# Attention and depthwise convolution on one core: the fourth pair's q and k copied through GpSimd's queue, two conv tiles added by accumulating transfers, one tap fewer before the last reciprocals

## The chip, the cores and the metric

The kernel runs on one core of a Trainium2 chip. The metric is the device time of one execution in microseconds. Before the change it is 2937.13 us, the median of three runs (2937.04 to 2937.74); the profiled execution took 2939.7 us, with a span of 2937.6 us in the trace. All times below that say where something stands are microseconds from the start of that span.

## The reference

The input x has 16 images of 384 channels and 32 x 32 pixels in float32. Two residual layers follow one another.

```python
# layer 0: attention with 8 heads of 48 channels over 1024 pixels
x = x + attention(group_norm(x, 32 groups), w_qkv, w_proj, b_proj)
# layer 1: one 7x7 filter per channel, padding 3, stride 1
x = x + depthwise_conv(group_norm(x, 32 groups), symmetrised(w_conv))
```

`group_norm` takes mean and variance over 12 channels and all pixels. `attention` is softmax(q k^T / sqrt(48)) v for each head, then a 384 x 384 projection with a bias. `symmetrised` is the mean of the filter and its three rotations by 90 degrees.

## The kernel before

An image is three tiles of 128 channels x 1024 pixels. The eight heads are worked as four **pairs**; a pair's two heads lie on rows 0 to 47 and 64 to 111 of a tile. A unit u is one pair of one image (u = 4 b + pair, 64 in all) and has 16 steps.

**TensorE, step by step.** A step makes scores (L463), ScalarE takes their exponential (L471), and TensorE multiplies by v (L479). Steps go in batches of eight: eight score steps, a slot for other work, eight steps with v, another slot. In the slots lie the q and k of the next pairs (L412, copied out of PSUM by ScalarE at L419), v (L438), the projection of the image before (L532, which reads o), and ScalarE's normalisations (L334). The matmuls of an image follow one another almost without a gap.

**The fourth pair's q and k.** Each of the three tiles that `qk_step` makes holds 48 rows for each of two heads and, in the rows left over (48 to 63 and 112 to 127), a third of the two heads of the fourth pair. `qk_rest` (L425 to L431) gathers these 6 x 16 rows into a tile of their own by six transfers of 128 KB from SBUF to SBUF. They are issued on SyncE's queue when the third q and k of an image have been emitted. Right after them the next image's x is loaded into the same buffer by three transfers (L155), on GpSimd's queue from image 2 on. The unit that reads the gathered rows begins 32 steps later.

**Softmax sums.** v carries a column of ones, so that one row of the product is the softmax sum. `sums_out` sends it through HBM into a compact tile (L497, L498, SyncE). VectorE takes the reciprocals (L504, `rec`), SyncE writes them to HBM (L506, inv<-rec) and, when that has landed, reads them back spread over 64 rows each (L509, inv<-inv). VectorE then multiplies o by inv (L515); after the fourth pair SyncE moves o's rows back to the packed order (L520), and the projection can read them. [...]

**VectorE.** Nearly all its work is the convolution: 49 instructions ("taps", L597) per tile, each a multiply-add of a shifted tile into x1. An order written by a small planner decides where everything else stands between the taps: `after(wait, cost, f)` puts f into the order when VectorE's planned clock gets there, and `catch_up` fills the time between with taps. The planner's clocks are fixed estimates.

**The end.** Four tiles of the last two images, `PE_TILES` = (14,2), (14,1), (15,2), (15,1), are convolved on TensorE (L705), of (14,1), called `SHARED`, only the last four pixel rows. `conv_on_pe_end` (L717 to L721) adds the PSUM result to x1 on VectorE (L720), and `conv_end` (L610) sends x1 to the output on GpSimd's queue. The tile (15,0) is convolved on VectorE into two accumulators that are added last (L860). In `fast_finish` the last pair is divided without going through HBM: two matmuls (L558) spread the sums, VectorE takes a 128 x 512 reciprocal (L560) and multiplies (L561), TensorE finishes the projection (L569), VectorE adds the residual (L578) and takes statistics (L234), TensorE averages these over groups (L302), and then the last image's tiles are normalised, stored and read back shifted (L674, L681) for TensorE. Two taps stand before the second L560 (L1140).

The pools that matter: `tpool` has 2 buffers of 128 x 1024 (squares and inv), `ps_s` 3 PSUM tiles of 128 x 1024, `xpool` 1 buffer for x.

Of the kernel before, what the change touches and what calls it, by code (L numbers as in the profile page):

```python
# [10 lines left out]
F32 = mybir.dt.float32  # L11
I32 = mybir.dt.int32
AF = mybir.ActivationFunctionType
ALU = mybir.AluOpType
AX = mybir.AxisListType

P = 128
# [27 lines left out]
def kernel(  # L45
# [25 lines left out]
    nc = tc.nc  # L71

    B, C, H, W = x.shape
    N = H * W
# [35 lines left out]
    def run(general):  # L110
        tag = "g" if general else "f"
        with ExitStack() as stack:
# [3 lines left out]
            def pool(name, bufs, **kw):  # L116
                return stack.enter_context(tc.tile_pool(name=f"{name}_{tag}", bufs=bufs, **kw))
# [8 lines left out]
            tpool = pool("tpool", 2)  # L126
# [10 lines left out]
            xds, shs, pss, mats, psums = {}, {}, {}, {}, {}  # L137
            PE_K = [NK - 1, NK - 2]

            PE_TILES = [(b, k) for b in (B - 2, B - 1) for k in PE_K]  # L140
            SHARED = None if general else (B - 2, PE_K[1])
# [3 lines left out]
            def flat(t):  # L145
                return t.rearrange("p h n -> p (h n)")
# [274 lines left out]
            def qk_rest(b):  # L421

                u = NP * b + NK
                qks[u] = qkpool.tile([P, 2, N], F32, tag="qk", name=f"qk_{u}")
                for t in range(NK):  # L425
                    for j in range(2):
                        r = 64 * j
                        nc.sync.dma_start(
                            qks[u][r + 16 * t : r + 16 * t + 16],
                            qks[NP * b + t][r + D : r + 64],  # L430
                        )  # L431
# [123 lines left out]
            def divide_at_once(u, h):  # L555
                half = os_[u][:, h * HALF : (h + 1) * HALF]
                ps = ps_o.tile([P, HALF], F32, tag="acc", name=f"ps_sum_{u}_{h}")
                nc.tensor.matmul(ps, lhsT=late["masks"][:, 7, :], rhs=half, start=True, stop=True)  # L558
                inv = tpool.tile([P, N], F32, tag="t", name=f"inv_{u}_{h}")[:, 0:HALF]
                nc.vector.reciprocal(inv, ps)  # L560
                nc.vector.tensor_tensor(half, half, inv, ALU.mult)  # L561

            def proj_part(b, o, ts):
                if o not in pps:
                    pps[o] = psum(f"ps_proj_{b}_{o}")
                for t in ts:
                    lhsT = wp[:, t, o * P : (o + 1) * P] if t < NK else late["w3"][:, o * P : (o + 1) * P]
                    for h in range(2):
                        nc.tensor.matmul(  # L569
                            pps[o][:, h, :],  # L570
                            lhsT=lhsT,
                            rhs=os_[NP * b + t][:, h * HALF : (h + 1) * HALF],
                            start=(t == 0),
                            stop=(t == NP - 1),
                        )

            def residual(b, o):
                nc.vector.scalar_tensor_tensor(  # L578
                    halves(x1s[b, o]), pps.pop(o), bp[:, o : o + 1], halves(x1s[b, o]), ALU.add, ALU.add
                )  # L580
# [9 lines left out]
            def conv_tap(b, k, dy, dx, dst=None):  # L590
                (oy, iy), (ox, ix) = region(dy, dx)
                if (b, k) == SHARED:
                    oy = slice(oy.start, min(oy.stop, SPLIT))
                    iy = slice(iy.start, oy.stop - oy.start + iy.start)
                dst = x1s[b, k] if dst is None else dst
                acc = dst.rearrange("p (h w) -> p h w", w=W)[:, oy, ox]
                nc.vector.scalar_tensor_tensor(  # L597
                    acc,
                    xn1s[b, k].rearrange("p (h w) -> p h w", w=W)[:, iy, ix],
                    wsym[:, k, dy + PAD, dx + PAD : dx + PAD + 1],  # L600
                    acc,
                    ALU.mult,
                    ALU.add,
                )

            def conv_end(b, k):
                if (b, k) == SHARED and not late.get("shared"):
                    late["shared"] = True
                    return
                nc.gpsimd.dma_start(  # L610
                    out[b, k * P : (k + 1) * P].rearrange("p h w -> p (h w)"), x1s.pop((b, k))
                )
# [104 lines left out]
            def conv_on_pe_end(b, k):  # L717
                c = slice(SPLIT * W if (b, k) == SHARED else 0, N)
                dst = x1s[b, k][:, c]
                nc.vector.tensor_tensor(dst, flat(pss.pop((b, k)))[:, c], dst, ALU.add)  # L720
                conv_end(b, k)  # L721

            def exact_step(u, i):
# [95 lines left out]
            def us_tap(dy, dx):  # L819
                late_us = 0.02 if clock > last_image else 0.0  # L820
                rows = H - abs(dy)
                if tuple(active[0][0:2]) == SHARED:
                    rows = min(H - max(0, dy), SPLIT) - max(0, -dy)
                return (rows * (W - abs(dx)) + (128 if len(active) > 1 else 268)) / 955 + late_us

            def tap():

                while len(active) < NK and chains:
                    active.append([*chains.popleft(), 0])
                if not active:  # L830
                    return 0.0
                b, k, n = active[0]
                if (b, k) == LONE:
                    active.append(active.pop(0))
                    return tap_of_two(b, k, active[-1])
                took = us_tap(*TAPS[n])
                conv_tap(b, k, *TAPS[n])
                c = active.pop(0)
                c[2] += 1
                if c[2] < len(TAPS):  # L840
                    active.append(c)
                else:
                    conv_end(b, k)
                return took

            def tap_of_two(b, k, c):

                n = c[2]
                c[2] += 1
                if n == 1:  # L850
                    late["sum2"] = opool.tile([P, N], F32, tag="o", name=f"sum2_{b}_{k}")
                    nc.vector.tensor_scalar(
                        late["sum2"], xn1s[b, k], wsym[:, k, PAD, PAD : PAD + 1], None, ALU.mult
                    )
                elif n < len(TAPS):

                    tn = n if n > 1 else 1
                    conv_tap(b, k, *TAPS[tn], late["sum2"] if n % 2 else None)
                else:
                    nc.vector.tensor_tensor(x1s[b, k], x1s[b, k], late["sum2"], ALU.add)  # L860
                    active.remove(c)
                    conv_end(b, k)
                return (950 + 128) / 955
# [246 lines left out]
            def conv_piece(n=0):  # L1110
                nonlocal clock
                b, k, h, part = pe_conv[n]
                del pe_conv[n]
                while (b, k, h, 1) not in shs and pe_loads:
                    loads(1)
                conv_on_pe(b, k, h, part)
                clock += 2.0 if (b, k) == SHARED else 6.2
                if part == 1:
                    loads(2)
                if (h, part) == (1, 1):  # L1120
                    after(6.0, 1.2, lambda: conv_on_pe_end(b, k))
# [13 lines left out]
            def fast_finish(b):  # L1135
                nonlocal clock, vclock
                late["tail"] = b == B - 1

                proj_part(b, 0, (NP - 2,))
                tap(), tap()  # L1140
                divide_at_once(NP * b + NP - 1, 1)
                for o in range(1, NK):
                    proj_part(b, o, (NP - 2,))
                x1_stats[b] = Stats(f"x1_{b}")
                tap(), tap()
                for o in range(NK):
                    proj_part(b, o, (NP - 1,))
                    residual(b, o)
                    x1_stats[b].channels(x1s[b, o], o)
                clock += 2 * US_PROJ + 1.0  # L1150
                vclock = clock + 4.0
# [14 lines left out]
            for b, n0, size in [  # L1166
# [35 lines left out]
                if ending:  # L1202
                    catch_up(clock)
                    assert not invs and not waiting
                    fast_finish(b)
                else:
                    other(n0 + size, True)
# [4 lines left out]
                if b == B - 1:  # L1212
# [10 lines left out]
                    if once("ones", r >= 32):  # L1223
                        t = opool.tile([P, N], F32, tag="o", name="masks_1")
# [74 lines left out]
```

## Time and profile before

| what | value | where |
|---|---|---|
| time | 2937.13 us | median of 3 runs |
| TensorE busy with matmuls | 2900.6 us, 99% | busy times |
| VectorE busy | 2575.7 us, 88% | busy times |
| ScalarE busy | 1442.0 us, 49% | busy times |
| GpSimd busy | 204.4 us, 7% | busy times |
| DMA engines, mean | 58 GB/s | the line of DMA shares |
| software queue (GpSimd's), hardware queue q1 (SyncE's) | 12.9% and 10.0% of the engines' span | DMA queues |
| qk copies, per image | 6 of 128 KB, issue median 587 ns, longest 3310 ns | line L428 |
| accumulating loads from GpSimd (L547) | issue 873 ns, landing 5.5 us | line L547 |

In the timeline an engine's name with a q (SPq, ACTq) is its queue issuing transfers; a number in square brackets is how long the engine stood idle before an instruction, with what ended the wait. In the chain of work each piece is what the next one waited for. Busy shares are means over stages with different limits, so the stages have to be looked at one by one.

### The profile page before, as it was taken

What the parts mean: (1) busy time and instruction counts of PE and PEld (TensorE: products, weight loads), DVE (VectorE), ACT (ScalarE), POOL (GpSimd) and SP (SyncE); (2) the same over time, 40 slices, a digit from 0 to 9 for tenths busy, and PEclk for the clock granted to TensorE, in tenths of its full rate; (3) what the DMA queues carried; (4) which work ended last, traced back from release to release, by engine and by line L of the source; (5) the groups of instructions that cost most, each with busy time, mean ns of one, the idle gap of its engine ahead of it and who ended that gap; (6) DMA issues with size and microseconds to landing.
All of it is one profiled execution on the core that took longest, in us unless ns stands there. A gap on an engine that the chain in (4) does not pass through costs nothing. (4 is left out here: it accounts for less than half of the span.)

```text
span 2937.6 us, 30293 instructions
## 1 busy us (share of the span) xinstructions
PE 2900.6 (99%) x11554; PEld 1171.1 (40%) x11554; DVE 2575.7 (88%) x2558; ACT 1442.0 (49%) x1724; POOL 204.4 (7%) x304
## 2 busy tenths in 40 slices
PE   8999999999999999999999999999999999999997
PEld 4343343434434343343434434343343434334332
DVE  5312998989999898999989999898999989899898
ACT  2545445464454545545464554546546365554510
POOL 3110004000100001000000100000010000100000
PEclk9999999999999999999999999999999999999998
DMA  7422022220302213022220301213031221301423
GB/s 298 116 26 62 16 35 77 41 63 21 82 16 42 69 23 82 16 43 62 42 62 24 83 21 35 69 29 75 16 64 41 42 63 28 83 16 35 119 65 110
DMA packets 72540, 169.84 MB, mean 58 GB/s; under 512 B 30416, under 2 KB 32352, under 8 KB 70848
## 3 DMA queue, kind: packets, MB, share of 16 engines
q0 software_dynamic: 29456, 96.08, 12.9%
q1 hardware_dynamic: 41328, 68.44, 10.0%
q10 hardware_dynamic: 1600, 3.28, 0.5%
q8 instruction: 93, 1.52, 0.2%
q14 instruction: 63, 0.52, 0.1%
HBM read 119.92 MB, written 29.36 MB: 51 GB/s over the span
## 5 line engine op out<-in xcount | busy, mean ns | idle before, releaser
L597 DVE SCALAR_TENSOR_TENSOR x<-xn,wsym,x 128x899 f32<-128x899 f32 (+11 forms) x2181 | 2371.7, 1165 | 105.4 <-ACT xn L334 105.4
L471 ACT ACTIVATE e<-ps_s 128x1024 f32<-128x1024 f32 x1024 | 952.3, 1054 | 54.8 <-PE ps_s L463 51.8
L463 PE MATMUL ps_s<-qk 48*128 48x512 f32 x4096 | 915.0, 596 | 2.2 <-ACT qk L419 2.2
L479 PE MATMUL acc<-e,v 128*64 128x512 f32 x4096 | 907.2, 595 | 0.0
L463 PEld LDWEIGHTS ps_s<-qk 48*128 48x128 f32 x4096 | 375.5, 185 | 537.9 <-ACT e L471 259.8
L479 PEld LDWEIGHTS acc<-e,v 128*64 128x64 f32 x4096 | 283.0, 137 | 608.2 <-issue 598.8
L412 PE MATMUL ps_qk<-x,wqk 128*128 128x512 f32 x1152 | 507.9, 597 | 2.4 <-DVE x L330 2.4
L490 ACT COPY o<-acc 128x512 f32<-128x512 f32 x128 | 75.2, 587 | 602.6 <-PE acc L479 602.6
L412 PEld LDWEIGHTS ps_qk<-x,wqk 128*128 128x128 f32 x1152 | 217.0, 191 | 289.6 <-issue 287.1
L438 PE MATMUL ps_v<-wv,x 128*128 128x384 f32 x768 | 252.0, 488 | 0.0
L532 PE MATMUL ps_proj<-o,wp 128*128 128x512 f32 x540 | 234.3, 592 | 1.5 <-DMA o<-o 1.5
L419 ACT COPY qk<-ps_qk 128x1024 f32<-128x1024 f32 x96 | 96.4, 1006 | 240.5 <-PE ps_qk L412 240.5
L438 PEld LDWEIGHTS ps_v<-wv,x 128*128 128x128 f32 x768 | 144.6, 190 | 109.6 <-ACT e L471 12.1
L515 DVE TENSOR_TENSOR o<-o,inv 128x1024 f32<-128x1024 f32 x63 | 77.1, 1224 | 115.1 <-DMA inv<-inv 79.3
L547 POOL DMA_DIRECT2D x<-in_x x45 | 39.2, 871 | 1831.4 <-ACT x L540 1698.8
L532 PEld LDWEIGHTS ps_proj<-o,wp 128*128 128x128 f32 x540 | 102.4, 190 | 128.1 <-issue 123.5
L447 ACT COPY v<-ps_v 128x384 f32<-128x384 f32 x128 | 55.1, 483 | 185.6 <-PE ps_v L438 185.6
L540 ACT ACTIVATE x<-ps_proj,bp 128x1024 f32<-128x1024 f32 x45 | 50.1, 1113 | 184.7 <-PE ps_proj L532 184.7
L334 ACT ACTIVATE xn<-x,sc_x 128x1024 f32<-128x1024 f32 x46 | 53.8, 1231 | 98.3 <-DMA sc_x<-gr_x 67.6
L705 PE MATMUL ps_conv<-sh,mat 128*32 128x480 f32 (+7 forms) x784 | 73.0, 527 | 1.5 <-DMA sh<-xd 1.5
L504 DVE RECIPROCAL rec<-sums 128x16 f32<-128x16 f32 x63 | 15.6, 248 | 54.3 <-DMA sums<-sum 54.3
L265 ACT ACTIVATE sq_x<-x,x_bs 128x1024 f32<-128x1024 f32 x45 | 51.2, 1139 | 21.0 <-DVE x_bs L947 21.0
(118 smaller groups left out, 517.6 us busy)
## 6 DMA issues: line engine op xcount, KB each, us to landing
x<-in_x POOLq DMA_DIRECT2D x90, 512.0 KB, 5.7
inv<-inv SPq DMA_DIRECT2D x126, 256.0 KB
out<-x POOLq DMA_DIRECT2D x48, 512.0 KB, 7.3
xs<-in_x POOLq DMA_DIRECT2D x42, 512.0 KB, 5.9
qk<-qk SPq DMA_DIRECT2D x96, 128.0 KB
o<-o SPq DMA_DIRECT2D x90, 64.0 KB
sh<-xd SPq DMA_DIRECT2D x36, 160.0 KB
sh<-xd ACTq DMA_DIRECT2D x20, 160.0 KB
```

The lines of the kernel that those rows point to most:

```text
L412: nc.tensor.matmul(ps[:, h, :], lhsT=wqk[:, k, s, t, :], rhs=xns[b][:, k, h * HALF : (h + 1) * HALF], start=(k == 0), stop=(k == NK - 1),)
L419: nc.scalar.copy(halves(qks[u][:, s, :]), ps)
L438: nc.tensor.matmul(ps[:, j, 0:C], lhsT=xns[b][:, k, t * P : (t + 1) * P], rhs=wv[:, k, :], start=(k == 0), stop=(k == NK - 1),)
L447: nc.scalar.copy(dst.rearrange("p (h d) -> p h d", d=D + 1)[:, :, 0:D], ps[:, j, 0:C].rearrange("p (h d) -> p h d", d=D),)
L463: nc.tensor.matmul(ps[:, j, :], lhsT=qks[u][r, 1, i * P : (i + 1) * P], rhs=qks[u][r, 0, h * HALF : (h + 1) * HALF], start=True, stop=True,)
L471: nc.scalar.activation(es[n], ps, AF.Exp, scale=SCALE)
L479: nc.tensor.matmul(accs[u, h][64 * j : 64 * j + 64, :], lhsT=v_of(u, i, j), rhs=e[:, j, :], start=(i == 0), stop=(i == NT - 1),)
L490: nc.scalar.copy(os_[u][:, h * HALF : (h + 1) * HALF], accs.pop((u, h)))
L515: nc.vector.tensor_tensor(os_[u], os_[u], invs.pop(u), ALU.mult)
L532: nc.tensor.matmul(ps[:, h, :], lhsT=wp[:, t, o * P : (o + 1) * P], rhs=os_[NP * b + t][:, h * HALF : (h + 1) * HALF], start=(t == 0), sto ...
L597: nc.vector.scalar_tensor_tensor(acc, xn1s[b, k].rearrange("p (h w) -> p h w", w=W)[:, iy, ix], wsym[:, k, dy + PAD, dx + PAD : dx + PAD + 1],
L705: nc.tensor.matmul(pss[b, k][CH * i : CH * (i + 1), h, :].rearrange("p (y x) -> p y x", x=W)[:, y0:, ox], lhsT=mats[k][:, i, d0 * KS + dx ...
```

## The change

Three edits. First, `qk_rest` issues its six copies on GpSimd's queue in place of SyncE's, so that SyncE's queue isn't held up by them. Second, for the tiles (14,2) and (15,2) ScalarE copies the PSUM result into a tile of `tpool`, and a transfer that accumulates, issued by GpSimd, adds it to x1 in place of VectorE; the output transfer then waits for that transfer. (14,1) and (15,1) stay with VectorE. Third, one tap instead of two stands in front of the second reciprocal of `fast_finish`; the tap isn't dropped, the planner puts it in later.

```diff
                     for j in range(2):
                         r = 64 * j
-                        nc.sync.dma_start(
+                        nc.gpsimd.dma_start(
                             qks[u][r + 16 * t : r + 16 * t + 16],
                             qks[NP * b + t][r + D : r + 64],
                         )
...
                 dst = x1s[b, k][:, c]
-                nc.vector.tensor_tensor(dst, flat(pss.pop((b, k)))[:, c], dst, ALU.add)
+                src = flat(pss.pop((b, k)))[:, c]
+                if (b, k) in (SHARED, PE_TILES[-1]):
+                    nc.vector.tensor_tensor(dst, src, dst, ALU.add)
+                else:
+
+                    t = tpool.tile([P, N], F32, tag="t", name=f"conv_{b}_{k}")
+                    nc.scalar.copy(t, src)
+                    nc.gpsimd.dma_start(dst, t, accum_op=ALU.add)
                 conv_end(b, k)
...
                 proj_part(b, 0, (NP - 2,))
-                tap(), tap()
+                tap()
                 divide_at_once(NP * b + NP - 1, 1)
```

## The prediction

> **What bounds the kernel now.** I read the busy times first, then the chain that ended last, then the timeline of the stages that the three edits touch. TensorE is busy 99% of the span, and from one load of x to the next (L155) most images take 175.10 us whatever else happens, so until the last image TensorE sets the pace and only its stalls can be won or lost. The end is different. The chain of work from 2829.55 on runs like this:
>
> ```profile
> 2829.55 3.27 DVE inv L560
> ...
> 2833.66 6.25 PE ps_proj L569 x10
> ...
> 2853.73 6.26 DMA sh<-xd
> 2860.00 0.24 issue
> 2860.24 10.74 PE ps_conv L705 x93
> ...
> 2878.42 1.14 DVE x L720
> ...
> 2902.80 1.13 DVE x L720
> ...
> 2923.27 1.24 DVE x L860
> ```
>
> It starts with the second reciprocal of the last pair on VectorE, goes over to TensorE and the shifted loads, and from 2872 to the last output is VectorE alone, tap after tap. Two of its links are the additions L720 that the change takes away. TensorE ends its last convolution at 2917.45 and VectorE its last instruction at 2925.63, so VectorE is the one to relieve. Why is the reciprocal so late?
>
> ```profile
> 2819.91 9.64 DVE L597 SCALAR_TENSOR_TENSOR x<-xn,wsym,x 128x930 f32<-128x930 f32 x9
> 2829.47 3.35 DVE L560 RECIPROCAL inv<-ps_sum 128x512 f32<-128x512 f32 x1
> 2824.67 1.02 PE L558 MATMUL ps_sum<-o,masks 128*128 128x512 f32 x2
> 2828.96 1.02 PE L569 MATMUL ps_proj<-o,mat 128*128 128x512 f32 x2
> 2833.66 0.70 PE L569 MATMUL ps_proj<-o,mat 128*128 128x512 f32 x1 [3.68 <-DVE o L561]
> ```
>
> Its input is ready at 2824.67 + 1.02 = 2825.69, but taps are in front of it until 2829.47: VectorE is 3.78 us behind, and TensorE stands for 3.68 us. VectorE's last stall before that is at the first inv of the last image, and from there to the reciprocal it is never idle, so the whole of that lag comes from here:
>
> ```profile
> 2724.33 7.67 SPq L428 DMA_DIRECT2D qk<-qk  x6
> 2732.10 0.53 SPq L506 DMA_DIRECT2D inv<-rec  x1
> 2740.03 1.12 SPq L509 DMA_DIRECT2D inv<-inv  x2
> 2728.13 0.24 DVE L504 RECIPROCAL rec<-sums 128x16 f32<-128x16 f32 x1
> 2744.67 1.23 DVE L515 TENSOR_TENSOR o<-o,inv 128x1024 f32<-128x1024 f32 x1 [6.45 <-DMA inv<-inv]
> ```
>
> rec is done at 2728.37, but SyncE is inside the six copies until 2732.0, and the 8 KB of inv<-rec then need 7.9 us behind them. Without copies on the way the same path is short: at 2658.33 the issue of inv<-rec is followed by inv<-inv after 1.43 us, and rec to L515 takes 2664.27 - 2658.05 = 6.2 us.
>
> [...] from 2721 to 2725 the outputs of GpSimd's queue alone move 406 GB/s, from 1330 to 1335, when x's load shares the engines with two qk copies, the table of stretches shows 180 GB/s at a DMA share of 0.98. [...] the trace has accumulating loads at L547, 5.5 us to land, but none from SBUF.
>
> **The copies.** From SyncE six issues per image go away (median 587 ns each, 3.5 us; with the wait for the third copy of ScalarE they span 10 us). inv<-rec in the last image can be issued at 2728.4 instead of 2732.1[...]. inv must land by 2738.2 (= 2744.67 - 6.45) for the full gain: 9.8 us after rec, against 6.2 us on a free path and with some 2 MB of other transfers under way. I take 6.45 with a lower bound of 3. A first reciprocal, at 2810.78, has its input at 2804.47 + 1.12 = 2805.6 and so passes on at most 5.2 us; that still suffices, as the second needs 3.74 - 1.03 = 2.7.
>
> In images 1 to 14 VectorE waits 3 to 6 us at the same place, and then about 5 us for ScalarE's xn at the next image, where a gain is lost again. Only two stalls of TensorE hang on it: 0.69 and 0.77 us at 1092 and 1443, where the projection waits for o. There rec stands behind taps, 8 us and more after its sums were sent for, so a VectorE that is 4 us ahead removes both: -1.5 us. A third stall, 1.05 us at 273.55, comes from ScalarE waiting 7.52 us for a scale whose small transfer runs beside the first qk copies; on GpSimd's queue they come after it. I count half: -0.5 us.
>
> What it adds is on GpSimd: six issues, at the 530 ns of an x load 3.2 us per image, on an engine busy 7%. Four of them go out while it waits idle (5.98 us before L155 at 1325.07). The last two wait for ScalarE's copy L419, which ends 0.75 us after the load could start, and take 1.06 us, so behind them **x is issued 1.9 us later**. ScalarE normalises x at L334 after eight exponentials, and here is the slack:
>
> ```profile
> 1325.88 7.44 ACT L471 ACTIVATE e<-ps_s 128x1024 f32<-128x1024 f32 x8
> 1334.85 1.24 ACT L334 ACTIVATE x<-x,x_sc 128x1024 f32<-128x1024 f32 x1 [1.53 <-DMA x<-in_x]
> 1336.38 2.53 ACT L334 ACTIVATE x<-x,x_sc 128x1024 f32<-128x1024 f32 x2 [0.30 <-DMA x<-in_x]
> 1338.91 0.59 ACT L490 COPY o<-acc 128x512 f32<-128x512 f32 x1
> ```
>
> Its waits for x in the 14 images are 1.28, 0.38, 1.41, 1.88, 1.73, 1.52, 0.63, 0.47, 0.38 and five near zero. The image with 1.73 takes 175.10 us all the same, so about 1.7 us are free. Is x later by the 1.9 us? Now it is issued first, runs at about 340 GB/s, and then collides with the two copies and falls to 180. [...] I take no loss, with bounds from 0 to 2 us of delay.
>
> **The additions.** Two L720 leave VectorE's chain: 1.14 + 1.13 = 2.27 us. ScalarE gets two copies of 128 x 1024 out of PSUM, about 1.0 us each as at L419, at a time when it does nothing but issue loads. GpSimd gets two accumulating issues of about 0.9 us and stands until each has landed, 5 to 8 us, before it can issue that tile's output. Behind it in its queue is only the next output: for (15,2) the addition stands at 2902.73, so its output can go at about 2912, and the next outputs come after 2920. PSUM is freed about as before. I put all this at nothing.
>
> **The tap.** The reciprocal moves up by one tap, 1.03 us, but the tap comes back at the end. With VectorE late, the chain moves by -1.03 and the end by +1.03; with VectorE early it costs 1.03, since the reciprocal then waits for TensorE anyway.
>
> **The sum at the end.** With inv early the reciprocal starts at about 2825.73, TensorE's projection at 2830.0 (its own earlier matmuls end at 2829.98), 3.66 us sooner. Everything down to 2872 follows TensorE and moves with it, VectorE's stalls of 2.75, 1.67, 1.01 and 1.78 us included. VectorE ends at 2925.63 - 3.66 + 1.03 - 2.27 = 2920.73, so -4.9 us. With -1.5 and -0.5 this makes -6.9 us: 2937.1 - 6.9 = 2930.2.
>
> **The rivals.** (1) *inv's wait stays*: other transfers hold it as long. For it: in the last image 1 MB of stores lies in SyncE's ring and the residual's loads move into the same time. Against it: 3.7 us of the delay are plain issue order. Then the tap nets to nothing, and 2937.1 - 2.3 = 2934.8 is left. A mixture, with x late by 1 us, lies in the same place: the five waits above 1.2 would exceed 1.7 by 4.3 us together, 2934.5. (2) *GpSimd's queue makes x late*. For it: [...] SyncE's copies took up to 3.3 us each to issue[...]. With 2 us of delay the nine waits exceed 1.7 by 12.4 us and the five others by 0.3 each: 13.9 us of stalls, 2930.2 + 13.9 = 2944.1, slower than before. Against it: the collision above.
>
> **How the numbers follow.** The forecast gets 0.58, rival 1 with the mixture 0.28, rival 2 0.14. The forecast itself may be 3 us better, if the stalls at 273 and of two whole images (0.93 and 1.21 us over 175.10) go entirely; so the range is 2927 to 2938, with rival 2 left out. 0.2% is 5.9 us, or 2931.3, and the forecast is near it: faster 0.57, same 0.30, slower 0.13.
>
> **What would show it.** SyncE should issue inv<-rec within 0.5 us of rec in each image; the stall of 6.45 us before L515 should shrink below 3.5; the second L560 should start at about 2825.7 less the stalls saved earlier, and TensorE's 3.68 us should vanish; two L720 should be left, and VectorE's chain to the end should hold one tap more. Images should stay at 175.10 us between L155 issues, and ScalarE's waits for x at or below 15.3 us in all. The prediction is wrong if those waits grow beyond 1.7 us per image, if inv lands after 2742, or if the reciprocal finds another wait in front of it.

## The result and the profile after

The changed kernel takes 2927.76 us (median of 6 runs, 2926.58 to 2929.67) against 2937.1 us (2936.91 to 2939.47): the ratio is 0.9967, with a 95% interval of 0.9954 to 0.998, so 9.3 us faster. Forecast were 2930.2 us, 6.9 us faster.

The single profiled runs differ by more, 2925.8 against 2937.6 us of span, because the profiled run of before was itself 2.6 us above its median. So I compare tails, from a common mark: the end of the last matmul that spreads the sums (L558), which stands at 2825.69 before and at 2822.08 after. From there VectorE ends 99.95 us later before and 93.95 us later after, and the span ends another 11.99 and 9.81 us later. The two tails make 6.0 + 2.2 us; about 1 us is left for the 15 images ahead.

The path of the last image's inv in the timeline of the changed kernel (SyncE's queue, then VectorE):

```profile
2724.34 0.32 SPq L506 DMA_DIRECT2D inv<-rec  x1
2728.32 1.95 SPq L509 DMA_DIRECT2D inv<-inv  x2
2724.07 0.25 DVE L504 RECIPROCAL rec<-sums 128x16 f32<-128x16 f32 x1
2738.85 1.23 DVE L515 TENSOR_TENSOR o<-o,inv 128x1024 f32<-128x1024 f32 x1 [4.68 <-PE ps_s L463]
```

inv<-rec goes out 0.27 us after rec began, not 3.97 us; it lands in 4.0 us, not 7.9. But now inv<-inv takes 10.5 us from issue to use, where it took 4.6. The wait before L515 is still 4.68 us. (The engine named as releaser had long been done; it is the transfer.) What inv<-inv now meets stands in GpSimd's queue, where L1231 before and L1238 after load the residual of the last image, three transfers of 512 KB. Before:

```profile
2722.93 0.54 POOL L1231 DMA_DIRECT2D x<-in_x  x1 [1.57 <-DMA out<-x]
2724.32 0.54 POOL L1231 DMA_DIRECT2D x<-in_x  x1 [0.86 <-DMA out<-x]
2725.65 0.53 POOL L1231 DMA_DIRECT2D x<-in_x  x1 [0.79 <-DMA out<-x]
```

and after:

```profile
2724.78 0.96 POOL L428 DMA_DIRECT2D qk<-qk  x2 [5.45 <-ACT qk L419]
2725.73 1.62 POOL L1238 DMA_DIRECT2D x<-in_x  x3
```

The last of these loads lands at 2738.7 before and at 2738.0 after. Before, inv<-inv was issued when they were done, at 2740.03; after, at 2728.32, in the midst of them. What comes of it before the last reciprocal, VectorE first and then TensorE:

```profile
2815.18 7.51 DVE L597 SCALAR_TENSOR_TENSOR x<-xn,wsym,x 128x868 f32<-128x868 f32 x7
2822.61 3.35 DVE L560 RECIPROCAL inv<-ps_sum 128x512 f32<-128x512 f32 x1
2821.05 1.02 PE L558 MATMUL ps_sum<-o,masks 128*128 128x512 f32 x2
2826.80 4.56 PE L569 MATMUL ps_proj<-o,mat 128*128 128x512 f32 x10 [0.43 <-DVE o L561]
```

The reciprocal starts 0.53 us after its input instead of 3.79, TensorE's stall of 3.68 us is down to 0.43, and the same ten passes of the projection take 4.56 us and not 6.25. That last difference was not in the forecast. The table of stretches says what it is. Its columns are the stretch, its length, the busy time and count of TensorE, its weight loads, VectorE, ScalarE and GpSimd, then TensorE's granted clock and the DMA share and rate. Before:

```profile
2830.00:2833.60 3.60, 0.00 (x0) 0.00 (x0) 3.51 (x3) 0.00 (x0) 0.00 (x0) 1.00 0.00 0
2833.70:2838.00 4.30, 4.30 (x6) 1.79 (x7) 4.26 (x5) 0.00 (x0) 0.00 (x0) 0.60 0.00 0
```

and after:

```profile
2826.80:2831.20 4.40, 4.40 (x10) 1.81 (x10) 4.37 (x6) 0.00 (x0) 0.00 (x0) 1.00 0.00 0
```

After the stall of before, the granted clock fell to half for 3.41 us (0.60 over the stretch) and six passes took the time of ten. The second thing not forecast is at the very end, in the instructions that close the kernel. GpSimd's queue drains three times there, and the longest (the third number of the durations, in ns) lies on the path to the end of the span. Before and after:

```profile
L1295 POOLq DRAIN  x3: 46/103/4605, 2932.2 to 2937.3; - x3
```

```profile
L1302 POOLq DRAIN  x3: 46/103/2802, 2922.2 to 2925.6; - x3
```

1.8 us less. The other 0.4 us lies ahead of the drains: the first begins 6.6 us after VectorE's end before and 6.2 us after. x's load is the one place that lost. ScalarE in the image shown in the prediction:

```profile
1323.38 7.44 ACT L471 ACTIVATE e<-ps_s 128x1024 f32<-128x1024 f32 x8
1331.25 1.24 ACT L334 ACTIVATE x<-x,x_sc 128x1024 f32<-128x1024 f32 x1 [0.43 <-DMA x<-in_x]
1334.24 2.37 ACT L334 ACTIVATE x<-x,x_sc 128x1024 f32<-128x1024 f32 x2 [1.75 <-DMA x<-in_x]
```

The first tile is there earlier (0.43 us of waiting, not 1.53), the second later. Over the 14 images whose x is loaded this way ScalarE waits 21.0 us for it instead of 9.6. (The 15.3 us that the prediction names hold another 5.7 us from the start of the kernel.) In the image with the longest wait, 3.2 us, TensorE took 175.66 us and not 175.10.

### The profile page after: what moved, and what is told of

The parts are those of the page before. It is cut to its first block, busy times and chain, and to the rows that moved or that the text cites. A ratio compares the mean times of both kernels' runs of the same rounds, so it can differ in the third digit from the quotient of the medians.

```text
span 2925.8 us, 30332 instructions
## 1 busy us (share of the span) xinstructions
PE 2897.7 (99%) x11554; PEld 1170.8 (40%) x11554; DVE 2573.2 (88%) x2556; ACT 1444.2 (49%) x1726; POOL 253.1 (9%) x402
## 4 chain that ended last, share of the span: by engine, by line
## 5 line engine op out<-in xcount | busy, mean ns | idle before, releaser
L515 DVE TENSOR_TENSOR o<-o,inv 128x1024 f32<-128x1024 f32 x63 | 77.4, 1228 | 59.5 <-DMA inv<-inv 47.5
L357 DVE BATCH_NORM_STATS2 bs_all<-xs 128x6 f32<-128x512 f32 x84 | 52.3, 683 | 19.0 <-DMA xs<-in_x 18.9
L334 ACT ACTIVATE x<-x,x_sc 128x1024 f32<-128x1024 f32 x42 | 51.1, 1266 | 21.0 <-DMA x<-in_x 21.0
```

What stands on the lines that cost most here:

```text
L334: nc.scalar.activation(dst, src, AF.Identity, bias=self.sc[:, k, 1:2], scale=self.sc[:, k, 0:1],)
L515: nc.vector.tensor_tensor(os_[u], os_[u], invs.pop(u), ALU.mult)
```

## The experiments

The theory with which they began: besides the terms of the prediction, the change gained because TensorE's stall no longer halves its clock. Rivals: the prediction's sum without a clock effect; or that whole images had gained. The table gives every run; the tail is measured as above, in us, and comes from one profiled run of each kernel. The times are medians beside those of the kernel before on the same chip; the chips differ, so differences of about 1 us between rows are safer read from the tails.

| run | us | before | ratio, 95% | reciprocal after its input | stall | projection's passes | VectorE's end | from there to the end | drain | GpSimd's transfers |
|---|---|---|---|---|---|---|---|---|---|---|
| before | | 2937.1 | | 3.79 | 3.68 | 6.26 | 99.95 | 11.99 | 4.61 | 285 |
| after | 2927.76 | 2937.1 | 0.9967 (0.9954 to 0.998) | 0.53 | 0.43 | 4.56 | 93.95 | 9.81 | 2.80 | 383 |
| copies alone | 2928.89 | 2936.84 | 0.9974 (0.9965 to 0.9984) | 0.60 | 0.49 | 4.56 | 95.09 | 9.66 | 2.64 | 381 |
| additions alone | 2934.86 | 2936.84 | 0.9992 (0.9984 to 1.0) | 3.42 | 3.32 | 6.06 | 97.13 | 12.28 | 4.77 | 287 |
| tap alone | 2935.82 | 2936.84 | 0.9998 (0.999 to 1.0006) | 2.63 | 2.52 | 6.26 | 99.93 | 12.04 | 4.61 | 285 |
| copies and additions, two taps | 2927.24 | 2936.84 | 0.9967 (0.9956 to 0.9978) | 0.32 | 0.21 | 4.56 | 92.57 | 9.84 | 2.80 | 383 |
| copies of the last image only | 2930.84 | 2936.54 | 0.9979 (0.9972 to 0.9987) | 0.04 | 0 | 4.56 | 93.15 | 12.90 | 5.26 | 293 |
| third copies only | 2930.38 | 2936.54 | 0.9979 (0.9971 to 0.9987) | 0.04 | 0 | 4.56 | 93.06 | 13.28 | 5.46 | 319 |
| five taps | 2929.03 | 2936.54 | 0.9976 (0.9967 to 0.9985) | 3.99 | 3.87 | 6.26 | 94.66 | 9.82 | 2.80 | 383 |
| loads on SyncE, two taps | 2926.43 | 2936.54 | 0.9964 (0.995 to 0.9977) | 0.04 | 0 | 4.56 | 91.86 | 9.57 | 2.56 | 380 |
| three taps | 2929.68 | 2937.99 | 0.997 (0.996 to 0.998) | 2.53 | 2.43 | 6.25 | 95.38 | 9.86 | 2.80 | 383 |
| four taps | 2929.73 | 2937.99 | 0.9973 (0.9964 to 0.9982) | 3.64 | 3.54 | 6.25 | 95.56 | 9.85 | 2.80 | 383 |
| 96 more transfers | 2933.56 | 2937.99 | 0.9987 (0.9979 to 0.9996) | 4.19 | 4.09 | 6.26 | 100.25 | 9.66 | 2.64 | 381 |

**The copies alone.** The kernel before with this edit:

```diff
-                        nc.sync.dma_start(
+                        nc.gpsimd.dma_start(
                             qks[u][r + 16 * t : r + 16 * t + 16],
```

> The kernel before with the first edit alone: the fourth pair's copies on GpSimd's queue, both taps and all four additions as before. Clock theory (what the changed kernel's trace suggests: TensorE's stall of 3.68 us before the last projection made its granted clock drop to half for 3.4 us, which costs some 1.5 us more, and the change shortened the stall below what triggers it): the stalls of TensorE at 273, 1092 and 1443 go, 3.6 us; VectorE is some 2.2 us earlier at the last reciprocal; the stall shrinks to about 1.5 us, the clock stays full, 1.5 us: together -7.3 us. Theory of the prediction (no clock effect, inv fully early): -2.0 and -3.7, so -5.7 us. Theory that the queue hardly matters and the other two edits made the gain: between 0 and -2 us.

8.0 us faster, so nearly the whole gain is in this edit. In the tail the reciprocal is 3.2 us nearer to its input and the passes take 1.7 us less: 4.9 us at VectorE's end. Another 2.3 us come at the close. The theory's total was close, but with a part that it got wrong, as the next two runs show.

**The additions alone.** The kernel before with the edit of `conv_on_pe_end` and nothing else.

> The kernel before with the second edit alone: the tiles (14,2) and (15,2) are added by accumulating transfers. All theories that put VectorE at the end of the chain: two instructions fewer, -2.3 us, with the trace of the rest unchanged, TensorE's stall of 3.7 us and its half clock included. Rival (the transfers and waits they bring delay the last outputs or hold PSUM): 0 or slower.

2.0 us faster in the medians, with an interval that just reaches 1.0; VectorE's end is 2.8 us earlier in the tail, of which 0.6 are a somewhat shorter stall and faster passes. The stall and the half clock are still there, as all theories had it. VectorE's end, 97.13 us behind the mark and not 99.95, shows no delay from the accumulating transfers.

**The tap alone.**

```diff
-                tap(), tap()
+                tap()
                 divide_at_once(NP * b + NP - 1, 1)
```

> The kernel before with the third edit alone: one tap instead of two before the second reciprocal of the last pair. Theory of the prediction: the chain moves by -1.03 us and the tap comes back at the end, so 0. Clock theory: the stall of TensorE shrinks from 3.68 to about 2.65 us, the clock no longer drops, the eight or so matmul passes after it take 0.43 us each and not 0.85: -1.5 us. Rival to the clock theory (the slow passes have another cause than the length of the stall[...]): they stay slow, 0.

The tail is the same to 0.02 us and the ratio is 0.9998 with 1 inside its interval. The prediction's reckoning of this edit held. The clock theory as I had put it failed: a stall of 2.52 us, shorter than I thought necessary, also halves the clock.

```profile
2828.42 5.83 PE L569 MATMUL ps_proj<-o,mat 128*128 128x512 f32 x9 [2.52 <-DVE o L561]
```

```profile
2828.40:2833.00 4.60, 4.58 (x7) 2.01 (x8) 4.52 (x6) 0.00 (x0) 0.00 (x0) 0.63 0.00 0
```

The first line is from the timeline, the second from the table of stretches with the clock 0.63. Cut more finely, the table shows that the half clock does not begin where the stall ends:

```profile
2828.42:2829.45 1.03, 1.03 (x3) 0.55 (x4) 1.03 (x2) 0.00 (x0) 0.00 (x0) 1.00 0.00 0
2829.48:2832.88 3.40, 3.40 (x6) 1.32 (x5) 3.37 (x4) 0.00 (x0) 0.00 (x0) 0.50 0.00 0
```

Here it begins 1.05 us after TensorE has resumed. With the additions alone it begins 0.36 us before, so that part of it falls into the stall, and the ten passes take 6.06 us and not 6.26. This run held a second surprise: none of TensorE's stalls at 273, 1092 and 1443, although all of its images are worked as before. With the additions alone only the one at 1092 is left. So those stalls come and go from run to run.

**Copies and additions with both taps.** The changed kernel with the third edit undone.

> The changed kernel with the two taps of before, so the first two edits together. Clock theory: the reciprocal is one tap later, TensorE stalls about 1.5 us instead of 0.43, the clock stays full in both, and the tap that no longer stands at the end pays for it: the same as the changed kernel within 0.5 us, -9.4 us. Theory of the prediction (VectorE so early that the reciprocal waits for TensorE anyway): one tap less at the end for nothing, 1.0 us better than the changed kernel. Theory that the third edit is a third of the gain: 3 us worse than it.

As fast as the changed kernel within what can be told (0.9967 both). In the tail it is 1.4 us better, 0.2 of it because the reciprocal stands nearer to its input. That fits the theory of the prediction: with the reciprocal near its input, the third edit costs what its tap costs at the end. The reciprocal is near even with two taps because inv came 1.3 us earlier against the common mark than in the changed kernel.

**Copies of the last image only.**

```diff
-                        nc.gpsimd.dma_start(
+                        (nc.gpsimd if b == B - 1 else nc.sync).dma_start(
                             qks[u][r + 16 * t : r + 16 * t + 16],
```

> The changed kernel, but only the last image's six copies go through GpSimd's queue; those of images 0 to 14 stay on SyncE's. The gain of the copies is now thought to have three parts in the tail and little elsewhere: VectorE 2.2 to 3.5 us earlier at the last reciprocal, TensorE's half clock avoided (1.7 us), and 2.0 us at the very end, where GpSimd's closing drain takes 2.6 to 2.8 us instead of 4.6 to 4.8 in the traces that have all copies on its queue. Theory A (the stalls at 273, 1092 and 1443 belong to the profiled run of before and not to the kernel, since the run with the tap edit alone lacks them): the first two parts stay, images 0 to 14 lose nothing; 2928 if the drain follows what GpSimd did in the last image, 2930 if it follows how many transfers it issued in all (drain about 4.7 us). Theory B (whole images gain from the copies as well): 1.5 to 3.6 us slower than that, with TensorE's stalls back.

The tail up to VectorE's end keeps all of its gain, 93.15 us; six copies out of 96 make it. The time is 3.1 us longer than the changed kernel's (on another chip), and the drain alone is 2.5 us longer, 5.26 us. No stall of TensorE at 273, 1092 or 1443 is back. That is theory A, with a drain that follows neither guess. What is left for the images 0 to 14 is about 1 us: the changed kernel gains 9.3 us, 8.2 of them in the tail, this one 5.7 us, with 5.9 in the tail.

**The third copies only.** The same place, with `t == NK - 1` as the condition: of each image's six copies only the two that wait for the third q and k go through GpSimd.

> The changed kernel, but only the two copies of each image that wait for the third q and k go through GpSimd's queue; the four others stay on SyncE's. Theory that SyncE's wait for that last copy is what holds inv<-rec up: the reciprocal path keeps most of its gain, VectorE is 2 us or more earlier in the last image, TensorE's clock stays full. Theory that the ring's load matters (four copies and 1 MB of stores ahead of inv<-rec in SyncE's ring): inv<-rec lands 3 us or more later than in the changed kernel, the gain at the reciprocal halves, the stall is 2 us or more and the clock may drop. For the closing drain: if it shrinks in proportion to the transfers on GpSimd's queue, about 4.1 us with 319 of them, between 4.77 with 287 and 2.80 with 383.

The first theory holds: inv<-rec is issued as early as with all six moved (0.27 us), VectorE's wait before L515 is 2.13 us, the reciprocal waits for TensorE. The four copies that stay on SyncE's queue do not hold inv<-rec up: inv<-inv follows it after 3.85 us (2723.76 to 2727.61), against 3.98 us in the changed kernel. The drain is 5.46 us with 319 transfers: it is not in proportion.

**The loads of the residual behind inv.** The changed kernel with two taps and this:

```diff
-                            nc.gpsimd.dma_start(
+                            nc.sync.dma_start(
                                 x1s[b, k], x[b, k * P : (k + 1) * P].rearrange("p h w -> p (h w)")
                             )
```

> An attempt at a better version: the changed kernel with two taps, and with the three loads of the last image's residual on SyncE's queue, so that they come behind inv<-inv and not beside it. In the changed kernel inv<-inv takes 10.5 us to land there, with 1.5 MB of these loads under way. Theory that they cause it: inv lands within 6 us of its issue, VectorE doesn't wait before L515 (4.68 us in the changed kernel), the last reciprocal waits for TensorE, no stall of TensorE beyond what the reciprocal itself takes; 0.5 us better than the version with two taps alone, or 2926.7. Rival (the copies and stores beside it cause it): the wait stays above 3 us and the time equals that of two taps alone, 2927.2.

```profile
2729.41 1.12 SPq L509 DMA_DIRECT2D inv<-inv  x2
```

```profile
2735.34 1.22 DVE L515 TENSOR_TENSOR o<-o,inv 128x1024 f32<-128x1024 f32 x1
```

```profile
2823.30 3.36 DVE L560 RECIPROCAL inv<-ps_sum 128x512 f32<-128x512 f32 x1 [1.31 <-PE ps_sum L558]
```

SyncE comes to the loads only at 2768, so they are gone from this stretch. inv is there 5.9 us after its issue, where the run with the same two taps took 9.2; L515 has no wait, and the reciprocal is the one that waits, 1.31 us, for TensorE. So most of what the changed kernel's 10.5 us have over the 4.6 of before are the residual's loads beside inv. The run with the third copies only agrees: there the last of these loads lands at 2734.5, and L515 starts at 2735.71. From the mark to the end of the span this version takes 1.0 us less than the one with two taps alone and 2.3 less than the changed kernel. The intervals of the times overlap, so that it is better is what one trace shows and not what the runs prove.

**Three, four and five taps** before the reciprocal, in the changed kernel.

> The changed kernel with five taps instead of one before the second reciprocal. The stall of TensorE grows from 0.43 to about 4.7 us. Clock theory: the granted clock drops to half for 3.4 us after it and the passes of the projection take twice as long, so VectorE's end is later by 4.2 (chain) - 4.2 (taps taken from the end) + 1.7 (clock) - 0.4 (the wait for TensorE that is used up): about 1.3 us over the changed kernel, and 2.6 over the one with two taps. Without a clock effect: 0.4 us faster than the changed kernel or equal.

> The changed kernel with three taps before the second reciprocal: a stall of TensorE between the 0.2 to 0.5 us that left its clock full and the 2.52 us (the tap edit alone) that halved it, about 1.3 us. If a stall this short leaves the clock full, VectorE's end stays at 92.6 us after the last spreading matmul (as with two taps) or earlier, and the time at 2927.2 or a little below; if it halves, 1.7 us more.

> The same with four taps: a stall of about 2.4 us. The tap edit alone had 2.52 us and a half clock for 3.4 us; if the length of the stall decides, this one has it as well: VectorE's end 94.3 us after the last spreading matmul, about 2928.9. [...]

All three have the half clock for 3.41 us and passes of about 6.25 us. Five taps end 0.7 us later in the tail than the changed kernel, with a stall of 3.87 us; the clock theory had 1.3 us for a stall of 4.7, the theory without a clock effect 0 or 0.4 us earlier, and the slow passes decide for the first. Three and four taps missed what they were made for: inv came 1.3 to 1.4 us later against the mark than in the run with two taps, and the stalls were 2.43 and 3.54 us instead of 1.3 and 2.4. Seven runs with stalls from 2.43 to 4.09 us before the projection have a half clock, six with 0.49 us or less don't. What lies between is in the same traces: in every run TensorE stands once more, before the convolution, for 1.1 to 1.7 us, and the clock stays full. The longest of these stalls, in the changed kernel, and the table of stretches behind it:

```profile
2851.91 8.36 PE L705 MATMUL ps_conv<-sh,mat 128*32 128x512 f32 x80 [1.71 <-DMA sh<-xd]
```

```profile
2851.90:2860.00 8.10, 8.09 (x80) 3.21 (x84) 8.10 (x9) 0.00 (x0) 0.00 (x0) 1.00 0.80 211
```

So in the tail 1.71 us left the clock full and 2.43 us was followed by half of it. The one stall between them, 2.38 us at the start of the kernel (it ends at 17.26 in the kernel before and at 17.15 in the changed one), doesn't decide: the clock stood at 0.50 when it began, since about 11.5 before and 14.3 after, and until about 21.7 and 21.2. TensorE's only stall from its first matmul at 5.09 up to that one had been 0.64 us, so there a half clock came without a stall of 2.43 us or more ahead of it.

**96 more transfers.** The kernel before, and in `qk_rest`:

```diff
+                for n in range(6):
+                    nc.gpsimd.dma_start(extra[n], b_proj[0:64].rearrange("(p c) -> p c", p=1))
```

> The kernel before (all copies on SyncE's queue) with 96 more transfers on GpSimd's queue that do nothing for the result: in qk_rest six loads of 64 elements each, one row, into tiles of their own. So GpSimd issues 381 transfers, as with the copies edit alone, but none of the copies. Theory that the closing drain depends on how many transfers GpSimd issued: drain 2.6 us in place of 4.6, and VectorE's end to the end of the span 9.7 us in place of 12.0; the rest of the tail as before (stall 3.7 us, half clock). Theory that rows or descriptors count, or what ran beside: drain elsewhere, 4.6 us or more. In time -2 us or 0; three of the six issues may also delay x by about 1 us.

```profile
L1298 POOLq DRAIN  x3: 46/108/2639, 2929.1 to 2932.3; - x3
```

The drain is 2.64 us, to the last digit that of the copies alone, with the same number of transfers and no copy among them. The rest of the tail is as before (stall 4.09 us, VectorE's end 100.25). So the closing drain goes with the number of transfers that GpSimd has issued, and 2 us of the change's gain have nothing to do with what the copies do. The packets of its queue, which are as many in both runs (32528), don't explain it: six copies, 192 packets, make the drain 0.49 us longer (287 to 293 transfers), two accumulating transfers, 288 packets, only 0.16 us (285 to 287). Between neighbours each transfer adds 0.08 us (these two steps, and 380 to 383), but 319 has 5.46 and 380 has 2.56, so it also falls somewhere; by which rule stays open. The kernel got 4.4 us faster in the medians, more than the 2.0 us of its tail; VectorE's waits before L515 in images 1 to 14 fell as well, from 62 to 29 us in all. What the remaining 2 us are was not followed up. As issues that copy nothing brought them, the 1 us that the changed kernel gains outside its tail can't be put down to the copies either.

## Why the prediction was right

**Mechanism.** The direction and the chain were right: inv freed from SyncE's queue, an earlier reciprocal, a shorter stall, two additions less on VectorE. The time lies inside the range, near its fast end. 9.3 us against 6.9 is the sum of these terms, of which the first four make the 6.0 us at VectorE's end:

| term | forecast, us | measured, us | from |
|---|---|---|---|
| reciprocal nearer to its input | -3.66 | -3.26 | 3.79 to 0.53 |
| tap back at the end | +1.03 | +1.2 | one against two taps: 1.4, less 0.2 of the reciprocal |
| two additions | -2.27 | -2.2 | copies alone against two taps: 2.5, less 0.3 of the reciprocal |
| TensorE's passes at full clock | 0 | -1.70 | 6.26 to 4.56 |
| VectorE's end to the end of the span | 0 | -2.2 | 11.99 to 9.81 |
| whole images | -2.0 | about -1.1 | remainder of 9.3, not shown by itself |

**What was mis-sized.** The step "I take 6.45 with a lower bound of 3" for inv failed: VectorE reached L515 only 2.2 us earlier against the common mark, and the wait that should have shrunk below 3.5 us was 4.68. The prediction saw that some 2 MB of other transfers would be under way and took the full gain all the same. Against the mark the residual's loads end 2.9 us later than before, as they stand behind the copies in GpSimd's queue, and inv<-inv goes out 8.1 us earlier, into them. Rival 1, *inv's wait stays*, was right about the cause and wrong in size. The reciprocal came near its input even so, because 2.2 us and the tap's 1.03 make up 3.2 of the 3.8 us: in this run the third edit stood in for what inv lacked. It wasn't needed in the two runs with two taps (copies alone, copies and additions): there inv came 1.0 and 1.3 us earlier against the mark. Whether that is the kernel or the single run wasn't tested.

**What was missing.** That TensorE's stall cost more than its length: 3.68 us of standing, and then 1.70 us in the ten passes. The trace of before had it in plain view, passes at twice the usual time and a granted clock of 0.60 right after the stall, and the prediction read only the stall. The seven stalls from 2.43 to 4.09 us were each followed by 3.41 us at half clock, the three shortest (2.43, 2.52 and 3.32 us) as well as the others, and in the 3.41 us just before each of these half clocks TensorE had stood for 2.3 to 3.1 us. What makes the clock fall, and what decides when the half begins, was not shown. The drain at the close was not in the prediction at all, and its dependence on a count couldn't be read from one trace.

**What was right by luck.** How near the total came, in part: 3.9 of the 9.3 us are the two terms that the prediction has at nothing, and its own terms came to 5.4 us instead of 6.9. Then the -1.5 and -0.5 us for three stalls of TensorE. They were read from one profiled run that lay 2.6 us above its median, and other runs of the same images have one of them or none. The common mark lies between 2821.61 and 2825.69 in the five runs whose images 0 to 14 keep all copies on SyncE, and between 2821.32 and 2823.27 in the eight others; the means differ by 1.3 us, the ranges overlap. A gain of about 1 us there is likely, not shown, and without a known cause.

**The rest.** x is issued 2.0 us later against ScalarE's exponentials (1.9 forecast). The author's estimate was that it loses nothing by this, and 2 us at most: its last tile lands where it did, 11.8 us after their start in both traces. ScalarE's waits for x grew by 11.4 us in all and exceed 1.7 us in seven of the 14 images, which the prediction had named as a sign of being wrong. Rival 2 didn't come all the same, because the slack is larger than the 1.7 us read from the trace of before: an image with 2.66 us of waiting still takes 175.10 us, as most do. The additions, the accumulating transfers and the wait of each output cost nothing on the path; the accumulating ones land 6.6 and 7.7 us after their issue has ended, within the 5 to 8 us allowed.

## What to carry to other kernels

A short transfer that an engine waits for belongs on a queue where nothing ahead of it waits for another engine: here inv<-rec went out 0.27 us after rec began instead of 3.97, and moving two of six copies was enough. When it is freed, ask which transfers are under way at its new, earlier time: here they were 1.5 MB of loads, and inv<-inv took 10.5 us instead of 4.6. Read the granted clock after every stall of TensorE, since removing the stall may also remove the slow stretch behind it (1.70 us of passes here), and take small stalls from more than one profiled run before counting them.

## What the runs showed of the hardware

The seven stalls of TensorE from 2.43 to 4.09 us before the projection were each followed by 3.41 us at half the granted clock, and the ten passes of 128 x 512 lasted 6.06 to 6.26 us instead of 4.56; stalls of 1.71 us and less, in the images and the tail, left it full. The half clock began between 0.4 us before and 1.1 us after TensorE resumed. At the start of the kernel the clock was at half for 10.2 us before the change and 6.8 us after it, with no stall above 0.64 us between TensorE's first matmul and the fall of the clock. GpSimd's longest closing drain took from 2.56 to 5.46 us, alike to 10 ns in kernels with the same number of its transfers (2.639 us twice with 381) and 0.08 us longer per transfer between neighbours. Two transfers of 256 KB (inv<-inv) took 5.9 us from issue to use with the residual's loads out of the way and 8.1 to 10.5 us with 1.5 MB of those loads beside them.
